# Attention and two quantized convolutions on one core: scores from stacks of two-part k and q, row sums shared with GpSimd, x kept in DRAM

## The chip, the cores and the metric

The kernel runs on one core of a Trainium2 chip. Time is device time in microseconds; lower is better. The engines are TensorE (PE, with its weight loads as PEld), VectorE (DVE), ScalarE (ACT), GpSimd (POOL) and SyncE (SP), which issues most DMAs.

## The reference

The input x is 4 images of 128 channels, 64x64. Layer 0 is self-attention over the 4096 positions of an image, with group norm in front and a residual behind. Layer 1 is a block of two 3x3 convolutions with weights quantized to 3 bits, each followed by batch norm, and a residual:

```python
x_norm = _group_norm(x, norm_w, norm_b)                  # 8 groups
qkv = einsum('oc,bchw->bohw', qkv_w, x_norm) + qkv_b
q, k, v = to_heads(...)                                  # 4 heads of d = 32
attn = softmax(einsum('bhid,bhjd->bhij', q, k) * d ** -0.5)
out = einsum('oc,bchw->bohw', proj_w, einsum('bhij,bhjd->bhid', attn, v)) + proj_b
x = x + out
...
out = relu(batchnorm(conv3x3(x, lsq_quantize(w1, alpha1)), gamma1, beta1))
out = batchnorm(conv3x3(out, lsq_quantize(w2, alpha2)), gamma2, beta2)
return relu(out + x)
```

All arrays are float32.

## The kernel before

*Staging.* All of x stays in SBUF as four padded images `xp` (66x66 a channel). Attention runs over 32 blocks (4 images times 8 blocks of 512 queries), and each block over 32 steps of 128 keys (`kt`). The steps form one long list, so the next block begins where the last one ends.

*A step.* `exp_step` makes the transposed scores of the four heads: four float32 matmuls (L279) with 32 rows of contraction each, the heads lying on different partitions, into two PSUM tiles `s` of two banks (three such tiles exist). In the trace a float32 matmul is two instructions. Two activations (L282) turn them into `p` tiles (128x2048, four buffers). No maximum is subtracted; instead the sums and their reciprocals are checked at the end (`worst`), and a general path would run if they were out of bounds. One step later `av_step` (L289) multiplies p with v into the accumulator `acc`, each head in its own 32 columns.

*Row sums.* `sum_step` (L302) adds the p tiles of four steps on VectorE (three adds of 128x2048), and `ones_step` (L306) sums the result over partitions with a matmul against ones, accumulated over eight groups in `l`.

*The end of a block.* `finish` copies acc and l, takes reciprocals in four pieces (L324), weighs, projects with `wp` (L333) and adds into xp (L335). These run as small tasks, one a step, in the next block (`side_work`).

*Projections.* `project_qkv` makes q, k and v of 512 positions. Image 0 is projected within block 0, and the next image within the last block of the one before. q, k and v stay in SBUF.

*Convolutions.* Bands of 16 rows are split into a high and a low part that float32r holds (L418, L419), and each 512 outputs take 18 float32r matmuls (L428): nine taps times two parts. ScalarE copies PSUM out (L459), VectorE takes the statistics. After the second layer the residual comes from xp (L486).

*Order.* Each engine works through its own list in order. The lists are laid out by a planner in the framework, which may run work ahead of its place in the program where its engine is free: the group norm statistics (L222) of images 1 to 3, called for in later blocks, all run between 17 and 47 us, and the weight quantization (`quant_tasks`, L188 to L202), called for after block 0, between 46.8 us and about 110 us.

Of the kernel before, what the change touches and what calls it, by code (L numbers as in the profile page):

```python
# [22 lines left out]
P = 128  # L23
# [14 lines left out]
GROUPED = 4  # L38
# [40 lines left out]
def _fast_body(ctx, tc, x, norm_w, norm_b, qkv_wt, qkv_b, proj_wt, proj_b,  # L79
# [10 lines left out]
    Q = H // 4  # L90
# [4 lines left out]


    xp = [const.tile([P, H + 2, PW], F32, name=f"xp{b}") for b in range(B)]

    def rows(t, r, n):
        return t[:, 1 + r : 1 + r + n, 1 : 1 + W]  # L100

    for b in range(B):
        for j in range(4):
            eng = nc.sync if b or j % 2 == 0 else nc.scalar
            eng.dma_start(out=rows(xp[b], j * Q, Q), in_=x[b, :, j * Q : (j + 1) * Q, :])

# [34 lines left out]
    for b in range(B):  # L141
        nc.gpsimd.memset(xp[b][:, 0, :], 0.0)
        nc.gpsimd.memset(xp[b][:, H + 1, :], 0.0)
        nc.gpsimd.memset(xp[b][:, 1 : H + 1, 0:1], 0.0)
        nc.gpsimd.memset(xp[b][:, 1 : H + 1, W + 1 : W + 2], 0.0)
# [13 lines left out]
    def quant_tasks(qp):  # L159
        tasks = []  # L160
        for i, (w, alpha) in enumerate(((w1, alpha1), (w2, alpha2))):
# [19 lines left out]
            for c in range(3):  # L181


                def taps(i=i, c=c, w=w, t=t):
                    wr = qp.tile([P, 3, P], F32, name=f"wr{i}{c}", tag="wr")
                    nc.sync.dma_start(out=wr, in_=w[:, 3 * c : 3 * c + 3, :])
                    q0 = qp.tile([P, 3, P], F32, name=f"q0{i}{c}", tag="q0")
                    nc.vector.tensor_scalar(q0, wr, t["inv"], -8.0, ALU.mult, ALU.max)  # L188
                    nc.vector.tensor_scalar(q0, q0, 8.0, None, ALU.min)
                    qh = qp.tile([P, 3, P], F32, name=f"qh{i}{c}", tag="qh")  # L190
                    nc.vector.tensor_scalar(qh, q0, SPLIT, None, ALU.add)
                    nc.vector.tensor_scalar(qh, qh, SPLIT, None, ALU.subtract)
                    ql = qp.tile([P, 3, P], F32, name=f"ql{i}{c}", tag="ql")
# [15 lines left out]
    with ExitStack() as att:  # L209
        qkvp = att.enter_context(tc.tile_pool(name="qkvp", bufs=NB + 1))  # L210
        pex = att.enter_context(tc.tile_pool(name="pex", bufs=2))
        quant = att.enter_context(tc.tile_pool(name="quant", bufs=1))
        pss = att.enter_context(tc.tile_pool(name="pss", bufs=3, space=PSUM))
        psa = att.enter_context(tc.tile_pool(name="psa", bufs=1, space=PSUM))

        norm, qs, ks, vs = {}, {}, {}, {}

        def norm_tasks(b):
            st = small.tile([P, NB, 6], F32, name=f"st{b}", tag="st")

            def stats(j):
                nc.vector.bn_stats(st[:, j, :], rows(xp[b], j * RB, RB))  # L222

            def combine():
                mv = small.tile([P, 2], F32, name=f"mv{b}", tag="mv")
                nc.vector.bn_aggr(mv, st.rearrange("p j s -> p (j s)"))

                gm = pss.tile([P, 2, FB], F32, name=f"gm{b}", tag="s")
                nc.tensor.matmul(gm[:, 0, 0:1], gavg, mv[:, 0:1], start=True, stop=True)
                mean = small.tile([P, 1], F32, name=f"mean{b}", tag="mean")  # L230
                nc.vector.tensor_copy(mean, gm[:, 0, 0:1])
                dv = small.tile([P, 1], F32, name=f"dv{b}", tag="dv")
                nc.vector.tensor_tensor(dv, mv[:, 0:1], mean, ALU.subtract)
                nc.vector.tensor_tensor(dv, dv, dv, ALU.mult)
                nc.vector.tensor_tensor(dv, dv, mv[:, 1:2], ALU.add)
                gv = pss.tile([P, 2, FB], F32, name=f"gv{b}", tag="s")
                nc.tensor.matmul(gv[:, 0, 0:1], gavg, dv, start=True, stop=True)
                r = rsqrt_eps(gv[:, 0, 0:1], f"gr{b}")
                a = small.tile([P, 1], F32, name=f"ga{b}", tag="ga")
                nc.vector.tensor_tensor(a, r, nw, ALU.mult)  # L240
                c = small.tile([P, 1], F32, name=f"gc{b}", tag="gc")
                nc.vector.tensor_tensor(c, mean, a, ALU.mult)
                nc.vector.tensor_tensor(c, nb, c, ALU.subtract)
                norm[b] = a, c

            return [lambda j=j: stats(j) for j in range(NB)] + [combine]
# [3 lines left out]
        def project_qkv(b, j):  # L250
            a, c = norm[b]
            xn = pex.tile([P, FB], F32, name=f"xn{b}_{j}", tag="xn")
            nc.vector.tensor_scalar(xn.rearrange("p (r w) -> p r w", w=W), rows(xp[b], j * RB, RB),  # L253
                                    a, c, ALU.mult, ALU.add)
            ps = pss.tile([P, 2, FB], F32, name=f"pqk{b}_{j}", tag="s")
            nc.tensor.matmul(ps[:, 0, :], wqkv[:, P : 2 * P], xn, start=True, stop=True)  # L256
            nc.tensor.matmul(ps[:, 1, :], wqkv[:, 0:P], xn, start=True, stop=True)
            k = ks[b, j] = qkvp.tile([P, FB], F32, name=f"k{b}_{j}", tag="k")
            q = qs[b, j] = qkvp.tile([P, FB], F32, name=f"q{b}_{j}", tag="q")
            nc.vector.tensor_scalar(k, ps[:, 0, :], bk, None, ALU.add)  # L260
            nc.vector.tensor_scalar(q, ps[:, 1, :], bq, None, ALU.add)  # L261
            ps = pss.tile([P, 2, FB], F32, name=f"pv{b}_{j}", tag="s")
            for i in range(KB):
                nc.tensor.matmul(ps[:, 0, i * P : (i + 1) * P], xn[:, i * P : (i + 1) * P],  # L264
                                 wqkv[:, 2 * P : 3 * P], start=True, stop=True)
            v = vs[b, j] = qkvp.tile([P, KB, P], F32, name=f"v{b}_{j}", tag="v")
            nc.vector.tensor_tensor(v, ps[:, 0, :].rearrange("p (i f) -> p i f", f=P),
                                    bv.unsqueeze(1).to_broadcast([P, KB, P]), ALU.add)
# [3 lines left out]
        def exp_step(blk, kt):  # L272
            b, qb = blk
            q, k = qs[b, qb], ks[b, kt // KB]
            c0 = (kt % KB) * P
            pt = pex.tile([P, HEADS, FB], F32, name=f"p_{b}_{qb}_{kt}", tag="pt", bufs=4)
            s = [pss.tile([P, 2, FB], F32, name=f"s_{b}_{qb}_{kt}_{i}", tag="s") for i in range(2)]
            for h in range(HEADS):
                nc.tensor.matmul(s[h // 2][:, h % 2, :], k[h * D : (h + 1) * D, c0 : c0 + P],  # L279
                                 q[h * D : (h + 1) * D, :], start=True, stop=True)  # L280
            for i in range(2):
                nc.scalar.activation(pt[:, 2 * i : 2 * i + 2, :], s[i], AF.Exp, scale=SCALE)  # L282
            return pt


        def av_step(blk, kt, pt, acc):
            v = vs[blk[0], kt // KB]
            for h in range(HEADS):
                nc.tensor.matmul(acc[h * D : (h + 1) * D, :], v[:, kt % KB, h * D : (h + 1) * D],  # L289
                                 pt[:, h, :], start=(kt == 0), stop=(kt == NK - 1))  # L290
# [3 lines left out]
        def sum_step(blk, kt, pts, sums):  # L294
            n = kt % GROUPED
            if n == 0:
                return
            if n == 1:
                sums[kt // GROUPED] = pex.tile([P, HEADS, FB], F32,
                                               name=f"r_{blk[0]}_{blk[1]}_{kt}", tag="r")  # L300
            r = sums[kt // GROUPED]
            nc.vector.tensor_tensor(r, pts[kt - 1] if n == 1 else r, pts[kt], ALU.add)  # L302

        def ones_step(g, sums, l):
            for h in range(HEADS):
                nc.tensor.matmul(l[h * D : (h + 1) * D, :], ones, sums[g][:, h, :],  # L306
                                 start=(g == 0), stop=(g == NK // GROUPED - 1))

        def finish(blk, acc, sums, l):

            b, qb = blk
            av = pex.tile([P, FB], F32, name=f"av{b}_{qb}", tag="av", bufs=1)
            nc.scalar.copy(av, acc)  # L313
            ls = pex.tile([P, FB], F32, name=f"ls{b}_{qb}", tag="ls", bufs=1)
            rc = pex.tile([P, FB], F32, name=f"rc{b}_{qb}", tag="rc", bufs=1)
            at = pex.tile([P, FB], F32, name=f"at{b}_{qb}", tag="at")

            def last_ones():
                ones_step(NK // GROUPED - 1, sums, l)
                nc.scalar.copy(ls, l)  # L320

            def invert(j):
                cs = slice(j * P, (j + 1) * P)
                nc.vector.reciprocal(rc[:, cs], ls[:, cs])  # L324

            def weigh():
                nc.vector.tensor_tensor(worst, worst, ls, ALU.max)  # L327
                nc.vector.tensor_tensor(worst, worst, rc, ALU.max)  # L328
                nc.vector.tensor_tensor(at, av, rc, ALU.mult)  # L329
# [13 lines left out]
        for t in norm_tasks(0):  # L343
            t()
# [5 lines left out]
        def second(n, kt):  # L350
# [7 lines left out]
            if kt % GROUPED == 2 and kt >= GROUPED:  # L358
                g = kt // GROUPED - 1
                if g == 0:  # L360
                    l[n] = psa.tile([P, FB], F32, name=f"l{n}", tag="l")
# [587 lines left out]
```

## Time and profile before

| what | value |
|---|---|
| time, median of three runs | 3031.2 us (3030.11 to 3031.35) |
| the profiled execution | 3029.39 us, span 3027.6 us |
| TensorE busy | 95% of the span |
| ScalarE, VectorE, GpSimd busy | 69%, 73%, 1% |
| granted TensorE clock, mean | 0.983 |
| copy of acc, first and last block | 161.7 us, 2688.5 us |

The span runs from the first to the last instruction. In lines of groups, the busy time and the mean duration of one instruction stand behind the first bar, and the idle time of the engine just before them, with what ended it, behind the second. In lines in order of time, the first number is the start in us and the second the duration. In lines of stretches, each engine has its busy time and instruction count, in the order PE, PEld, DVE, ACT, POOL, followed by the granted clock, the DMA share and GB/s.

### The profile page before, as it was taken

The page shows a single profiled execution, that of the slowest core. Times are in us where ns is not written, and L with a number is a line of the kernel's source. Part 1 is how long each engine was busy: PE and PEld are TensorE (multiplying, and loading weights), DVE is VectorE, ACT ScalarE, POOL GpSimd, SP SyncE. Part 2 cuts the span into 40 slices and gives each one's busy share as a digit, 9 for nine tenths or more (in the row PEclk, how much of TensorE's full clock was granted, in tenths as well). Part 3 has the DMA queues.
Part 4 walks back from the last instruction along what each step waited for, and adds up shares of the span by engine and source line. Part 5 has one row for each costly group of instructions (what it writes and reads, how often), then busy time and mean ns, then how long its engine had stood idle before and what let it go on. Part 6 is the DMA issues. An engine that isn't in the chain of part 4 may idle for free.

```text
span 3027.6 us, 45635 instructions
## 1 busy us (share of the span) xinstructions
PE 2884.3 (95%) x20050; PEld 928.2 (31%) x20050; DVE 2206.7 (73%) x1475; ACT 2100.7 (69%) x2209; POOL 18.5 (1%) x86
## 2 busy tenths in 40 slices
PE   5899999999999999999999999999999999989895
PEld 2222222223222222222222222232222222237773
DVE  8877777766777777767777777767777777763334
ACT  2488888856888888856888888757888888841223
POOL 1000000000000000000000000000000000000000
PEclk9899999999999999999999999999999999999997
DMA  6000000000000000000000000000000000000002
GB/s 124 9 1 1 1 1 1 1 1 1 1 1 1 1 1 1 1 1 1 1 1 1 1 1 1 1 1 1 1 1 1 1 1 1 1 1 1 1 0 113
DMA packets 36881, 21.30 MB, mean 7 GB/s; under 512 B 33777, under 2 KB 34545, under 8 KB 36673
## 3 DMA queue, kind: packets, MB, share of 16 engines
q1 hardware_dynamic: 32064, 16.91, 2.2%
q8 instruction: 159, 2.61, 0.4%
q10 hardware_dynamic: 4128, 1.05, 0.2%
q0 software_dynamic: 480, 0.33, 0.1%
q14 instruction: 50, 0.40, 0.0%
HBM read 9.90 MB, written 8.39 MB: 6 GB/s over the span
## 4 chain that ended last, share of the span: by engine, by line
PE 63%; DVE 28%; ACT 5%; issue 2%; DMA 1%; SPq 0%; DVEq 0%; POOL 0%; POOLq 0%; ACTq 0%
PE s L279 27%; PE acc L289 21%; DVE r L302 19%; PE ps L428 9%; PE l L306 5%; ACT p L282 5%; DVE rc L324 3%; DVE k L260 1%; DVE q L261 1%; DVE xp L335 1%; DVE at L329 1%; DVE worst L327 1%; DVE worst L328 1%; DMA out_dram<-y 0%; DVE st L222 0%
## 5 line engine op out<-in xcount | busy, mean ns | idle before, releaser
L282 ACT ACTIVATE p<-s 128x1024 f32<-128x1024 f32 x2048 | 1991.7, 1024 | 655.0 <-PE s L279 644.1
L279 PE MATMUL s<-q,k 32*128 32x512 f32 x8192 | 1293.6, 644 | 57.9 <-DVE q L261 47.0
L302 DVE TENSOR_TENSOR r<-r,p 128x2048 f32<-128x2048 f32 x512 | 1171.4, 2288 | 53.2 <-ACT p L282 9.2
L289 PE MATMUL acc<-p,v 128*32 128x512 f32 x8192 | 1100.9, 608 | 7.5 <-ACT av L313 7.5
L302 DVE TENSOR_TENSOR r<-p,p 128x2048 f32<-128x2048 f32 x256 | 586.7, 2292 | 541.8 <-ACT p L282 541.8
L279 PEld LDWEIGHTS s<-q,k 32*128 32x128 f32 x8192 | 411.5, 184 | 921.9 <-issue 548.5
L289 PEld LDWEIGHTS acc<-p,v 128*32 128x32 f32 x8192 | 162.1, 108 | 795.1 <-issue 761.7
L306 PE MATMUL l<-r,ones 128*32 128x512 f32 x2048 | 266.6, 592 | 1.8 <-DVE r L302 1.8
L459 ACT COPY cv<-ps 128x512 f32<-128x512 f32 x64 | 37.6, 588 | 208.3 <-PE ps L428 207.2
L428 PE MATMUL ps<-lo,wq 128*128 128x512 f32 x576 | 151.4, 408 | 11.6 <-DVE lo L419 11.6
L428 PE MATMUL ps<-hi,wq 128*128 128x512 f32 x576 | 148.4, 402 | 0.0
L428 PEld LDWEIGHTS ps<-lo,wq 128*128 128x128 f32 x576 | 110.4, 192 | 41.6 <-issue 12.1
L428 PEld LDWEIGHTS ps<-hi,wq 128*128 128x128 f32 x576 | 109.3, 190 | 29.4
L460 DVE BATCH_NORM_STATS2 st<-cv 128x6 f32<-128x512 f32 x64 | 44.3, 692 | 100.3 <-ACT cv L459 100.3
L306 PEld LDWEIGHTS l<-r,ones 128*32 128x32 f32 x2048 | 66.5, 110 | 155.3 <-issue 151.7
L324 DVE RECIPROCAL rc<-ls 128x128 f32<-128x128 f32 x128 | 108.2, 909 | 1.8 <-ACT ls L320 1.8
L478 ACT ACTIVATE t<-cv,bc,ba 128x1088 f32<-128x1088 f32 (+1 forms) x16 | 21.1, 1328 | 31.5 <-DVE lo L419 27.7
L418 DVE CAST hi<-t 128x1188 fp32r<-128x1188 f32 x16 | 12.5, 778 | 41.1 <-PE ps L428 39.7
L333 PE MATMUL po<-at,wp 128*128 128x512 f32 x64 | 36.9, 660 | 5.4 <-DVE at L329 5.4
L418 DVE CAST hi<-xp 128x1188 fp32r<-128x1188 f32 x16 | 12.3, 776 | 38.7 <-PE ps L428 38.7
L256 PE MATMUL pqk<-xn,wqkv 128*128 128x512 f32 x64 | 37.0, 660 | 3.0 <-DVE xn L253 3.0
L264 PEld LDWEIGHTS pv<-wqkv,xn 128*128 128x128 f32 x256 | 33.7, 192 | 15.6 <-issue 15.3
(98 smaller groups left out, 500.3 us busy)
## 6 DMA issues: line engine op xcount, KB each, us to landing
out_dram<-y SPq DMA_DIRECT2D x16, 512.0 KB, 2.7
xp<-in_x_dram SPq DMA_DIRECT2D x14, 512.0 KB, 7.7
wr<-in_L_conv_w_dram SPq DMA_DIRECT2D x6, 192.0 KB, 2.4
xp<-in_x_dram ACTq DMA_DIRECT2D x2, 512.0 KB, 10.5
wqkv<-in_L_conv_qkv_w_dram POOLq DMA_DIRECT2D x1, 192.0 KB, 6.6
bv<-in_L_conv_qkv_b_dram POOLq DMA_DIRECT2D x1, 64.0 KB, 7.2
wp<-in_L_conv_proj_w_dram POOLq DMA_DIRECT2D x1, 64.0 KB, 6.9
gamma<-in_L_conv_gamma_dram POOLq DMA_DIRECT2D x2, 0.5 KB, 6.5
```

What stands on the lines that cost most here:

```text
L256: nc.tensor.matmul(ps[:, 0, :], wqkv[:, P : 2 * P], xn, start=True, stop=True)
L264: nc.tensor.matmul(ps[:, 0, i * P : (i + 1) * P], xn[:, i * P : (i + 1) * P], wqkv[:, 2 * P : 3 * P], start=True, stop=True)
L279: nc.tensor.matmul(s[h // 2][:, h % 2, :], k[h * D : (h + 1) * D, c0 : c0 + P], q[h * D : (h + 1) * D, :], start=True, stop=True)
L282: nc.scalar.activation(pt[:, 2 * i : 2 * i + 2, :], s[i], AF.Exp, scale=SCALE)
L289: nc.tensor.matmul(acc[h * D : (h + 1) * D, :], v[:, kt % KB, h * D : (h + 1) * D], pt[:, h, :], start=(kt == 0), stop=(kt == NK - 1))
L302: nc.vector.tensor_tensor(r, pts[kt - 1] if n == 1 else r, pts[kt], ALU.add)
L306: nc.tensor.matmul(l[h * D : (h + 1) * D, :], ones, sums[g][:, h, :], start=(g == 0), stop=(g == NK // GROUPED - 1))
L324: nc.vector.reciprocal(rc[:, cs], ls[:, cs])
L333: nc.tensor.matmul(ps[:, 0, :], wp, at, start=True, stop=True)
L428: nc.tensor.matmul(ps, w[:, tap, :], part[:, j * RB + kh : j * RB + kh + RB, kw : kw + W], start=(n == 0), stop=(n == 2 * TAPS - 1))
L459: nc.scalar.copy(dst, ps)
L460: nc.vector.bn_stats(st[:, b * NB + j, :], dst)
```

## The change

*Scores.* q and k are each split into a high and a low float32r part. For each head, k stands four times 32 rows deep as (high, low, high, low) and q as (high, high, low, low), so that one float32r matmul with 128 rows of contraction gives the sum of the four products. A step's scores are four such matmuls.

*Stacks by way of DRAM.* The projection writes the parts and v to DRAM (five stores a chunk of 512 positions), and the stacks are loaded back with the heads side by side: four loads for k and one for v a chunk, four for q a block. All of these are issued by SP.

*Phases.* The program emits scores of three pairs of heads, then the weights of one step, then three more pairs, then the weights of two steps. There are six p buffers.

*Row sums.* In each block p tiles of ten steps (`POOLED`) are added on GpSimd (nine adds), the others on VectorE (21 adds); the two sums meet at step 29 (a 22nd add). The ones product runs once a block. `worst` is kept by GpSimd, with adds in place of maxima.

*Projections.* Chunks of the next image are spread over blocks 2 to 7 of the image before (two in blocks 2 and 3, then one a block), each a few pieces over four steps, in a PSUM bank of their own. Of image 0, three chunks are projected before the first step and five within block 0.

*x in DRAM.* Attention writes its result to DRAM (`y0`), which the first convolution loads back band by band, and the last step again as the residual. x is loaded in chunks where it is needed.

*Ends.* Quantization uses the tiles of the projection's stages and is called for in blocks 1 and 2 of the last image. The first two bands are loaded and split in the last block, and convolved around the finish of it.

```diff
-            for h in range(HEADS):
-                nc.tensor.matmul(s[h // 2][:, h % 2, :], k[h * D : (h + 1) * D, c0 : c0 + P],
-                                 q[h * D : (h + 1) * D, :], start=True, stop=True)
...
+    def scores(pair):
+        step, half = divmod(pair, 2)
...
+        s = pss.tile([P, 2, FB], F32, name=f"s{n}_{kt}_{half}", tag="s")
+        for i in range(2):
+            h = 2 * half + i
+            nc.tensor.matmul(s[:, i, :], k[:, h, c0 : c0 + P], q[:, h, :], start=True, stop=True)
+        nc.scalar.activation(pts[step][:, 2 * half : 2 * half + 2, :], s, AF.Exp, scale=SCALE)
...
+        def parts(what, bias, slot):
+            hi = stage.tile([P, FB], F32R, name=f"{what}h{b}_{j}", tag=f"{what}h")
+            lo = stage.tile([P, FB], F32R, name=f"{what}l{b}_{j}", tag=f"{what}l")
+            nc.vector.tensor_scalar(hi, ps[what], bias, None, ALU.add)
+            nc.vector.scalar_tensor_tensor(lo, ps[what], bias, f32(hi), ALU.add, ALU.subtract)
+            nc.sync.dma_start(out=kq[b, j][slot], in_=f32(hi))
+            nc.sync.dma_start(out=kq[b, j][slot + 1], in_=f32(lo))
...
+    def load_stack(t, b, j, slots):
+        for s, slot in enumerate(slots):
+            nc.sync.dma_start(
+                out=f32(t)[s * D : (s + 1) * D, :, :],
+                in_=kq[b, j][slot].rearrange("(h d) n -> d h n", d=D))
+
+    def load_kv(b, j):
+        ks[b, j] = stack_tile(f"k{b}_{j}")
+        load_stack(ks[b, j], b, j, (0, 1, 0, 1))
+        v = vs[b, j] = vpool.tile([P, KB, P], F32, name=f"v{b}_{j}", tag="v")
+        nc.sync.dma_start(out=v.rearrange("p i f -> p (i f)"), in_=kq[b, j][4])
...
+    POOLED = (1, 2, 4, 7, 10, 13, 16, 19, 22, 25)
+    MERGE = 29
...
+        if kt in POOLED:
+            if kt == POOLED[1]:
+                psum[n] = rpool.tile([P, HEADS, FB], F32, name=f"rp{n}", tag="rp")
+                nc.gpsimd.tensor_tensor(psum[n], pts[step - 1], pt, ALU.add)
+            elif kt > POOLED[1]:
+                nc.gpsimd.tensor_tensor(psum[n], psum[n], pt, ALU.add)
+        elif kt == 3:
+            rsum[n] = rpool.tile([P, HEADS, FB], F32, name=f"r{n}", tag="r")
+            nc.vector.tensor_tensor(rsum[n], pts[step - 3], pt, ALU.add)
+        elif kt > 3:
+            nc.vector.tensor_tensor(rsum[n], rsum[n], pt, ALU.add)
+        if kt == MERGE:
+            nc.vector.tensor_tensor(rsum[n], rsum[n], psum[n], ALU.add)
...
+        def weigh():
+            nc.vector.tensor_tensor(av, av, rc, ALU.mult)
+            nc.gpsimd.tensor_tensor(worst, worst, t["ls"], ALU.add)
+            nc.gpsimd.tensor_tensor(worst, worst, rc, ALU.add)
...
+        def store():
+            nc.vector.scalar_tensor_tensor(t["x"], t["o"], bp, t["x"], ALU.add, ALU.add)
+            nc.sync.dma_start(out=y0[b][:, qb * FB : (qb + 1) * FB], in_=t["x"])
...
+        if n + 1 < len(blocks) and qb < NB - 1:
+            add(2, "", lambda: load_q(b, qb + 1))
...
+            for j, kt in {2: ((0, 13), (1, 22)), 3: ((2, 13), (3, 22)), 4: ((4, 15),),
+                          5: ((5, 15),), 6: ((6, 15),), 7: ((7, 15),)}.get(qb, ()):
...
+                chunk(b + 1, j, kt, project_parts(b + 1, j, lambda xt=xt: xt[0]), False)
...
+    run_scores(2)
+    while at["step"] < steps:
+        for s, w in ((3, 1), (3, 2)):
+            run_scores(s)
+            run_weights(w)
...
+    def load_band(b, g):
+        raw[b, g] = t = band_tile(f"t0_{b}_{g}")
+        inner, lo, hi = border(t, g)
+        nc.sync.dma_start(out=inner, in_=y0[b].rearrange("p (h w) -> p h w", w=W)[:, lo:hi, :])
...
+            r = outs.tile([P, Q], F32, name=f"r{b}_{j}", tag="r")
+            nc.sync.dma_start(out=r, in_=y0[b][:, cs])
             y = outs.tile([P, Q], F32, name=f"y{b}_{j}", tag="y")
-            nc.vector.scalar_tensor_tensor(y, cv[b][:, j * Q : (j + 1) * Q, :], a2,
-                                           rows(xp[b], j * Q, Q), ALU.mult, ALU.add)
+            nc.vector.scalar_tensor_tensor(y, cv[b][:, cs], a2, r, ALU.mult, ALU.add)
```

## The prediction

> **What bounds the kernel now.** I read the busy shares first, then the slices, the groups, the order of time in one block, and the stretches by engine. All sums are made against the profiled execution: span 3027.6 us, 3029.4 us with what lies around it, 1.8 us under the median of 3031.2 us. I take 3.6 us as the step from a span to a median; 0.2% (6 us) is about what a measurement of this kernel can tell from no change.
>
> Busy shares and slices:
>
> ```profile
> PE 2884.3 (95%) x20050; PEld 928.2 (31%) x20050; DVE 2206.7 (73%) x1475; ACT 2100.7 (69%) x2209; POOL 18.5 (1%) x86
> ...
> PE   5899999999999999999999999999999999989895
> ...
> ACT  2488888856888888856888888757888888841223
> ```
>
> TensorE is full; ScalarE dips every ninth slice, between two batches; GpSimd does nothing. The groups (line, engine, busy us, mean ns, idle before them):
>
> ```profile
> L282 ACT ACTIVATE p<-s 128x1024 f32<-128x1024 f32 x2048 | 1991.7, 1024 | 655.0 <-PE s L279 644.1
> L279 PE MATMUL s<-q,k 32*128 32x512 f32 x8192 | 1293.6, 644 | 57.9 <-DVE q L261 47.0
> L302 DVE TENSOR_TENSOR r<-r,p 128x2048 f32<-128x2048 f32 x512 | 1171.4, 2288 | 53.2 <-ACT p L282 9.2
> ```
>
> ScalarE waits for scores (644 us). One step in order of time (start, duration):
>
> ```profile
> 217.19 1.14 PE L279 MATMUL s<-q,k 32*128 32x512 f32 x8
> 218.26 1.06 PE L289 MATMUL acc<-p,v 128*32 128x512 f32 x8
> 219.25 1.31 PE L279 MATMUL s<-q,k 32*128 32x512 f32 x8
> ```
>
> Scores 1.07, weights 0.99; ones add 0.97 in one step of four. A steady block, and one that projects the next batch:
>
> ```profile
> 161.70:239.10 77.40, 76.78 (x582) 20.02 (x578) 60.45 (x32) 63.08 (x67) 0.00 (x0) 1.00 0.00 1
> 628.00:746.00 118.00, 109.42 (x672) 35.51 (x666) 78.71 (x62) 63.72 (x67) 0.00 (x0) 0.97 0.00 1
> ```
>
> PE, its loads, DVE, ACT, POOL: 77.4 us with PE at 76.8; three blocks of about 118 us carry 3 x 40.6 = 122 us of projections. The copies of acc place the rest: block 0 ends at 161.7, the last at 2688.5, and 339.1 us of finish, convolutions and output follow. The 31 blocks between average 81.5 us.
>
> **The change part by part.**
>
> *Scores.* A step's eight instructions at 1.07 us become four one-pass products. The nearest row is the convolution, also fp32r over 128 rows, with a weight load each: nine start every 2.15 us.
>
> ```profile
> 2717.63 2.32 PE L428 MATMUL ps<-lo,wq 128*128 128x512 f32 x9
> 2719.78 2.31 PE L428 MATMUL ps<-hi,wq 128*128 128x512 f32 x9
> ```
>
> So 0.239 each, 0.956 a step. Over three steps: 12 x 0.239 = 2.87; weights 0.99 + 0.99 where scores follow, 0.89 where weights follow (215.33 to 216.22 has no change of form) = 2.87. The drain from a 128-row product into the weights isn't shown: 0 to 0.2, twice. 5.74 to 6.14 per three steps, so 61 to 66 a block.
>
> *Ones.* Eight groups become one: 7 x 0.97 = 6.8 us leave PE.
>
> *Projections.* 2.8 us of PE a chunk (656.03 to 658.83), now one a block on average, plus ones 1.0 and wp 1.1: PE needs 66 to 71 us a block. ScalarE, two exps per 1.94 us and two copies of 0.59, needs 63.3. With three score buffers and phases they cannot dovetail fully: 66 to 74, I take 70.
>
> *Row sums.* DVE: 24 adds become 21 and the merge, 22 x 2.29 = 50.4. Four reciprocals 3.6, av 0.69, residual 0.75, statistics 0.69, and per chunk 0.54 + 4 x 0.75 + 0.68 = 4.2 (the hi and lo passes): 60.3 us in all. Nine adds of 128x2048 go to POOL. No row prices one. Below: 2.29, were POOL as fast as DVE. Above: POOL's affine_select of 128x128 took 0.36 against 0.10 for 128x1 memsets, 2.05 ns an element of one input; doubled for two inputs, 8.5. I take the row itself, 2048 x 2.05 + 0.1 = 4.3 us: 38.7 a block; the two 512-wide adds into worst, 1.15 each, 2.3: 41 us. The Trainium skill (GPSIMD Engine Reference, 3.1) measures 4497 ns for this add and would make it 42.8.
>
> POOL's 41 us fit under 70, if POOL and DVE run side by side. The trace has one place that speaks on this: POOL memsets of 18 elements, 0.13 us in the open, but not while DVE casts:
>
> ```profile
> 2850.14 0.77 DVE L418 CAST hi<-t 128x1188 fp32r<-128x1188 f32 x1
> ...
> 2850.37 0.61 POOL L470 MEMSET t<- 128x18 f32 x1 [4.48 <-DVE lo L419]
> ...
> 2854.61 0.13 POOL L470 MEMSET t<- 128x18 f32 x1 [1.42 <-DVE lo L419]
> ```
>
> The first ends at 2850.98, 0.07 us after the cast (2850.91); the same at 2852.49. So the two engines share a way into SBUF, and one waits out the other's whole instruction. The memset then ended inside the next DVE TENSOR_TENSOR: that one lets POOL write. Whether it lets POOL read is not shown: POOL reads nothing beside such an add here. But the cast reads 1188 elements in 0.78 us and the TENSOR_TENSOR 2 x 1188 in 1.38: the same rate, as if by the same two paths. By that nearest row I take it that a DVE add and a POOL add exclude each other; the other end, no contact, is kept. The Trainium skill (SBUF — State Buffer, Who interferes with whom) says so outright: a DVE instruction with two SBUF inputs contends with a GpSimd one that reads SBUF, and whoever comes second waits for the whole of the first; the trace agrees for the cast, and no run here shows the add. By the rule alone, at the page's 4497 ns, the block is 98 us; without it 70.
>
> Taken in turns, a block needs 50.4 + 0.7 + 41 = 92; DVE's other 9 us hide in POOL's turns only when they stand at the head of its queue, say half: 97 us. Behind a waiting DVE add stand the chunk's hi/lo passes, the reciprocals and the residual, for which PE and SP wait; behind a waiting POOL add only the next. Both hold p buffers: six, so ScalarE stops when the adds are three or four steps late.
>
> *DRAM.* A block adds some 18 issues on SP, 0.33 us each (the output's stores): 6 us; 4.5 MB in 70 us or more is 64 GB/s, against 212 GB/s at the start, and loads come a block ahead. SP is in order; behind a load waiting for a k buffer stand the next q and residual, due 20 steps later: nothing. The first scores gain a store and a load, 2 x 2.7: at 32 us instead of 27. Bands of x (256-byte runs, 2.5 us to issue, 7.7 to land) hide behind the 8.6 us that a band convolves, two ahead.
>
> *Quantization.* 42 us of DVE lay in block 0 (46.8 to 103). It moves or is planned early again: 21 us in turns, half hidden.
>
> *End.* Two bands convolve beside the last finish: the 13.8 us from 2688.5 to 2702.3 go. The residual, once in SBUF, is 16 loads of 512 KB: 8.4 MB went out in 30 us, so 12 loads not yet in cost 22 us. Bounds: 0, and +54 if each load queues behind the store before it (16 x (2.7 + 1.28 + 1.15) = 82, against 28). Tail 339 - 14 + 22 = 347. Border memsets lie on POOL, idle there.
>
> *Sum.* 32 + 32 x 97 = 3104 + 10 (five chunks in block 0, 21 us of DVE, half hidden) + 21 + 347 = 3514; at the median, 3518. I say 3515.
>
> **The rivals.**
>
> *Side by side* (the other side). POOL's adds cost DVE nothing. 32 + 32 x 70 + 14 (five chunks on PE) + 22 (quantization over DVE's 10 us of slack in two blocks) + 347 = 2655; with 66 to 74, 2530 to 2785. It decides at (3027.6 - 410)/32 = 81.8 us a block, 12 over the free pace: 56 + 41f = 81.8, so when less than f = 0.63 of POOL's time is lost to DVE. For: POOL is idle, and the memset ran beside the TENSOR_TENSOR. Against: the equal read rates.
>
> *Shared by the element.* The path alternates and neither waits out an instruction. If half of POOL's 41 us hides, 56 + 20 = 76, up to 56 + 34 = 90: 2860 to 3290, either sign. For: the memset needed only the cast's end. Against: it waited for the whole of it.
>
> *The planner undoes the phases.* Engine order is planned (statistics of batches 1 to 3 already ran at 17 to 47 us). Alternating every step costs 0.1 to 0.3 us a step, 3 to 10 us a block: 2750 to 2980 without contact; nothing in turns.
>
> **How the numbers follow.** In turns 0.57; shared by the element 0.15, half of it faster; side by side, phases kept or not, 0.28. Faster 0.28 + 0.07 = 0.35, same 0.01, slower 0.64. In turns alone: 3350 to 3680 (block 92 to 102). Eight in ten must reach into side by side: 2620 to 3680 leaves out about a tenth at each end.
>
> **What would show it.** Right: DVE adds far over 2.29 us or with gaps that end at POOL's, POOL busy over 40 us a block, PE and ACT near 65% in all slices, blocks near 97 us. Score products starting every 0.24 us and no 118 us blocks hold in either case. Wrong if POOL and DVE adds overlap at their own lengths, or blocks stay under 80 us.

## The result, and the profile after

The changed kernel takes 3635.4 us (median of four runs, 3635.16 to 3635.71) against 3030.8 us before (four runs): 1.1995 times the time, 95% interval 1.1974 to 1.2016. The profiled execution is 3635.68 us, its span 3634.0 us at a mean granted clock of 0.909 (0.983 before).

Busy shares and three of the slice rows of the page of after:

```profile
PE 3014.7 (83%) x14162; PEld 1259.9 (35%) x14162; DVE 3159.2 (87%) x1411; ACT 2062.7 (57%) x2209; POOL 1748.3 (48%) x462
...
DVE  5999989997998989998998999998999999996333
ACT  2665566665665565665665566566556666661122
POOL 3554565564554555555554455555544556561000
```

The full engine is VectorE now, in every slice of the attention, with GpSimd about half busy beside it. ScalarE's dips at every ninth slice are gone: the projections are spread, as the change says. But its level is 5 to 6 tenths instead of 8.

The groups of the page of after (busy us, mean ns, then idle time before them):

```profile
L341 ACT ACTIVATE p<-s 128x1024 f32<-128x1024 f32 x2048 | 1950.1, 1032 | 1142.5 <-PE s L340 938.2
L364 DVE TENSOR_TENSOR r<-r,p 128x2048 f32<-128x2048 f32 x640 | 2367.2, 3699 | 117.9 <-ACT p L341 88.8
L359 POOL TENSOR_TENSOR rp<-rp,p 128x2048 f32<-128x2048 f32 x256 | 1374.4, 5369 | 706.2 <-ACT p L341 703.8
L340 PE MATMUL s<-q,k 128*128 128x512 f32 x4096 | 1285.7, 437 | 114.5 <-ACT p L341 101.3
...
L362 DVE TENSOR_TENSOR r<-p,p 128x2048 f32<-128x2048 f32 x32 | 102.8, 3213 | 103.5 <-ACT p L341 60.9
```

The same DVE add, with the same shapes, that took 2288 ns before has a mean of 3699. The 640 adds of L364 lie between 2219 and 6689 ns, with a median of 2293; 241 are over 2.5 us (minimum/median/maximum ns, first and last start in us):

```profile
L364 DVE TENSOR_TENSOR r<-r,p x640: 2219/2293/6689, 59.3 to 3293.7; 128x2048 f32<-128x2048 f32 x160
```

The chain that ended last, by engine and by line (shares of the span):

```profile
DVE 54%; PE 26%; issue 13%; ACT 4%; DMA 2%; POOL 1%; DVEq 0%; SPq 0%; POOLq 0%; ACTq 0%
```

and some of its longest pieces in order of time (start, us):

```profile
28.02 9.27 DMA kq<-kh
181.87 6.60 DVE r L364
...
1813.71 6.67 DVE r L364
1847.38 6.51 DVE r L364
```

The path runs through the long adds. Here is one stretch in order of time, VectorE and then GpSimd in the trace of after (start, duration):

```profile
1796.29 6.19 DVE L364 TENSOR_TENSOR r<-r,p 128x2048 f32<-128x2048 f32 x1
...
1803.27 5.81 DVE L364 TENSOR_TENSOR r<-r,p 128x2048 f32<-128x2048 f32 x1
...
1809.87 2.22 DVE L364 TENSOR_TENSOR r<-r,p 128x2048 f32<-128x2048 f32 x1
```

```profile
1795.74 4.59 POOL L359 TENSOR_TENSOR rp<-rp,p 128x2048 f32<-128x2048 f32 x1
1801.95 4.98 POOL L359 TENSOR_TENSOR rp<-rp,p 128x2048 f32<-128x2048 f32 x1 [1.62 <-ACT p L341]
1810.02 3.22 POOL L394 TENSOR_TENSOR worst<-worst,rc 128x512 f32<-128x512 f32 x1 [3.09 <-DVE rc L389]
```

Work out the ends. The first GpSimd add ends at 1800.33; the DVE add that began inside it ends at 1802.48, 2.15 us later, one whole add. The second GpSimd add began at 1801.95, while that DVE add still ran, and ends at 1806.93, 4.45 us after the DVE add's end, again about one whole add. The DVE add of 1803.27 ends at 1809.08, 2.15 after GpSimd's end. And the other way round: the small GpSimd add of 1810.02 ends at 1813.24, 1.15 after the DVE add of 1809.87 does (1812.09). Whoever comes second waits out the whole of the first, in both directions. Over the whole trace, of 710 TENSOR_TENSORs of DVE longer than 2 us, the 304 that meet no GpSimd instruction have a mean of 2.29 us, the 406 that meet one 4.62.

### The profile page after: what moved, and what is told of

Its sections match the earlier page's. It is cut to its first block, busy times and chain, and to the rows that moved or that the text cites. A ratio compares the mean times of both kernels' runs of the same rounds, so it can differ in the third digit from the quotient of the medians.

```text
span 3634.0 us, 35912 instructions
## 1 busy us (share of the span) xinstructions
PE 3014.7 (83%) x14162; PEld 1259.9 (35%) x14162; DVE 3159.2 (87%) x1411; ACT 2062.7 (57%) x2209; POOL 1748.3 (48%) x462
## 4 chain that ended last, share of the span: by engine, by line
DVE 54%; PE 26%; issue 13%; ACT 4%; DMA 2%; POOL 1%; DVEq 0%; SPq 0%; POOLq 0%; ACTq 0%
DVE r L364 46%; PE acc L352 8%; PE c L584 7%; PE s L340 7%; ACT p L341 3%; DVE r L362 2%; DVE r L366 1%; PE pq L280 1%; PE l L382 1%; DVE rc L389 1%; PE pv L293 1%; DMA r<-y 0%; DVE kl L286 0%; POOL rp L359 0%; DVE y L681 0%
## 5 line engine op out<-in xcount | busy, mean ns | idle before, releaser
L364 DVE TENSOR_TENSOR r<-r,p 128x2048 f32<-128x2048 f32 x640 | 2367.2, 3699 | 117.9 <-ACT p L341 88.8
L359 POOL TENSOR_TENSOR rp<-rp,p 128x2048 f32<-128x2048 f32 x256 | 1374.4, 5369 | 706.2 <-ACT p L341 703.8
L340 PE MATMUL s<-q,k 128*128 128x512 f32 x4096 | 1285.7, 437 | 114.5 <-ACT p L341 101.3
L352 PE MATMUL acc<-p,v 128*32 128x512 f32 x8192 | 1380.6, 633 | 0.0
L340 PEld LDWEIGHTS s<-q,k 128*128 128x128 f32 x4096 | 723.6, 197 | 1082.9 <-ACT p L341 601.7
L357 POOL TENSOR_TENSOR rp<-p,p 128x2048 f32<-128x2048 f32 x32 | 169.6, 5301 | 565.4 <-ACT p L341 413.6
L362 DVE TENSOR_TENSOR r<-p,p 128x2048 f32<-128x2048 f32 x32 | 102.8, 3213 | 103.5 <-ACT p L341 60.9
L584 PE MATMUL c<-lo,wq 128*128 128x512 f32 x576 | 152.1, 408 | 9.5 <-DVE lo L433 8.1
L382 PE MATMUL l<-r,ones 128*32 128x512 f32 x256 | 51.8, 868 | 121.2 <-DVE r L364 121.2
L584 PE MATMUL c<-hi,wq 128*128 128x512 f32 x576 | 149.0, 403 | 0.0
```

Source lines behind the costliest of these rows:

```text
L340: nc.tensor.matmul(s[:, i, :], k[:, h, c0 : c0 + P], q[:, h, :], start=True, stop=True)
L352: nc.tensor.matmul(acc[n][h * D : (h + 1) * D, :], v[:, kt % KB, h * D : (h + 1) * D], pt[:, h, :], start=(kt == 0), stop=(kt == NK - 1))
L357: nc.gpsimd.tensor_tensor(psum[n], pts[step - 1], pt, ALU.add)
L359: nc.gpsimd.tensor_tensor(psum[n], psum[n], pt, ALU.add)
L362: nc.vector.tensor_tensor(rsum[n], pts[step - 3], pt, ALU.add)
L364: nc.vector.tensor_tensor(rsum[n], rsum[n], pt, ALU.add)
```

## The experiments

The theory on record was "in turns": a two-input DVE add and a GpSimd add exclude each other, and their sum sets the block. Its rivals were that they run side by side and something else is slow, that they share by the element, and that the planner, which lays out each engine's order, breaks up the phases on PE. "Block" below is the mean distance between copies of acc. It is 81.5 us before and 100.9 after.

### What makes the adds long

**No adds on GpSimd.** The ten steps of `POOLED` are left out of the row sums, and so is the merge:

```diff
         if kt in POOLED:
-            if kt == POOLED[1]:
-                psum[n] = rpool.tile([P, HEADS, FB], F32, name=f"rp{n}", tag="rp")
-                nc.gpsimd.tensor_tensor(psum[n], pts[step - 1], pt, ALU.add)
-            elif kt > POOLED[1]:
-                nc.gpsimd.tensor_tensor(psum[n], psum[n], pt, ALU.add)
+            pass
...
-        if kt == MERGE:
-            nc.vector.tensor_tensor(rsum[n], rsum[n], psum[n], ALU.add)
```

> The nine POOL adds and the merge left out (ten tiles of a block are missing from the row sums), the 21 DVE adds stay. In turns: DVE adds at 2.29 us, DVE 58 us a block, the pace falls to what PE and ScalarE allow, 68 to 74 us a block, 2600 to 2780 us. If the stacks, phases or DRAM are what costs: blocks stay over 85 us and the time over 3150.

Measured: 2923.6 us, 0.9654 of before [0.9635, 0.9673]. The DVE adds are at 2.29 us again and the block is 78.5 us. The group of adds in this run:

```profile
L360 DVE TENSOR_TENSOR r<-r,p 128x2048 f32<-128x2048 f32 x640 | 1468.2, 2294 | 342.7 <-ACT p L341 324.1
```

So the GpSimd adds and the merge together are worth 3635.4 - 2923.6 = 712 us, more than the whole loss of 605. But 78.5 is above the 68 to 74 that was expected of a free block; the next section takes that up.

**GpSimd writes only.** Each GpSimd add becomes two memsets of the same tile (the sums of those tiles are lost; GpSimd stays busy for 3.64 us instead of 4.59):

```diff
-                nc.gpsimd.tensor_tensor(psum[n], psum[n], pt, ALU.add)
+                nc.gpsimd.memset(psum[n], 0.0)
+                nc.gpsimd.memset(psum[n], 0.0)
```

> Each POOL add replaced by two memsets of the same 128x2048 tile, so that POOL writes as much but reads nothing (the row sums lack ten tiles); the DVE adds and the merge stay. If a two-input DVE add excludes only a POOL instruction that reads: DVE adds stay at 2.29 us, blocks at 70 to 76, 2640 to 2820 us. If any POOL work in SBUF excludes it: DVE adds average over 3 us and the time stays over 3200.

Measured: 2949.5 us, 0.9739 [0.972, 0.9759], block 79.2. The groups of this run:

```profile
L366 DVE TENSOR_TENSOR r<-r,p 128x2048 f32<-128x2048 f32 x640 | 1468.1, 2294 | 330.5 <-ACT p L341 311.1 <-DVE r L366 0.5 <-ACT av L378 0.5
L361 POOL MEMSET rp<- 128x2048 f32 x256 | 466.1, 1821 | 12.8
```

GpSimd is busy for 1200.7 us of this run, and the DVE adds keep 2294 ns (12 of 640 are over 2.5 us). A busy GpSimd isn't what costs; one that only writes passes a two-input DVE add. It doesn't pass every DVE instruction: the normalization of a chunk (`xn<-x`, one 128x512 tile from SBUF), 0.54 us by itself, takes up to 2.09 us here:

```profile
L276 DVE TENSOR_SCALAR xn<-x,ga,gc x24: 536/680/2089, 228.7 to 1849.6; 128x512 f32<-128x512 f32 x24
```

Why this run takes 26 us more than the one before, which also lacks the merge, was not tested.

**DVE reads one input.** 20 of the 21 adds of DVE become reductions of p alone, into four columns (the sums of those tiles are then wrong); GpSimd adds as in the changed kernel:

```diff
-            nc.vector.tensor_tensor(rsum[n], rsum[n], pt, ALU.add)
+            nc.vector.tensor_reduce(rsum[n][:, :, 0], pt, AX.X, ALU.add)
```

> POOL's nine adds stay; 20 of the 21 DVE adds become reductions of the same p tile along its rows into four columns (one SBUF input, the same 2048 elements; the row sums are left out). In turns by the read path: the reductions keep their own length, 2.2 to 2.4 us, POOL's adds fall to 4.2 to 4.6 us beside them, blocks at 70 to 78, 2640 to 2860 us. If POOL and DVE exclude each other whatever DVE reads, or if POOL's adds are that slow by themselves: POOL adds stay over 5 us, or DVE's over 3, and the time over 3300.

Measured: 2998.2 us, 0.99 [0.988, 0.992], block 81.0. That is above the range expected, with PE as the bound again (83% of its chain). Its groups:

```profile
L364 DVE TENSOR_REDUCE r<-p 128x4 f32<-128x2048 f32 x640 | 1458.0, 2278 | 288.3 <-ACT p L341 268.5 <-DVE r L364 0.9
L359 POOL TENSOR_TENSOR rp<-rp,p 128x2048 f32<-128x2048 f32 x256 | 1192.3, 4657 | 547.3 <-ACT p L341 545.7
```

```profile
L359 POOL TENSOR_TENSOR rp<-rp,p x256: 4497/4589/6522, 55.7 to 2637.5; 128x2048 f32<-128x2048 f32 x128
```

The reductions read the same tiles in the same time as the adds (2278 ns, at most 2293) and meet GpSimd's adds without a loss on either side: GpSimd's add now has a median of 4.59 us, its own length. Together the two runs name the resource: DVE's second input and GpSimd's reads. One thing more changed with the reductions: they write four columns where the adds write 2048. That DVE's writes are not what collides can be seen in the trace of after. The residual `x<-po,bp,x` (L404) reads one tile from PSUM and one from SBUF and writes all 512 columns; 13 of its 32 instructions begin while a GpSimd add runs, and the longest of the 32 takes 751 ns:

```profile
L404 DVE SCALAR_TENSOR_TENSOR x<-po,bp,x x32: 737/739/751, 188.4 to 3305.9; 128x512 f32<-128x512 f32 x32
```

DVE's second input and GpSimd's reads are also what the Trainium skill names (SBUF — State Buffer, Who interferes with whom): a DVE instruction with two SBUF inputs contends with a GpSimd one that reads, not with one that only writes, and a reduction never contends. The runs here agree on all three, with 3699 against 2294 and 2278 ns. One SBUF input alone doesn't make a DVE instruction safe, though. In the trace of after 12 of the 24 normalizations (L276) begin while GpSimd adds and take 1.48 to 4.81 us; the other 12 take 0.53 to 0.55:

```profile
L276 DVE TENSOR_SCALAR xn<-x,ga,gc x24: 532/1012/4807, 256.8 to 2338.3; 128x512 f32<-128x512 f32 x24
```

So this instruction collides with GpSimd's adds and with its memsets, as the cast of the trace before did with a memset. What sets it apart from the reduction was not tested.

**GpSimd reads one input.** Each GpSimd add becomes a copy of p (the sums again lost):

```diff
-                nc.gpsimd.tensor_tensor(psum[n], psum[n], pt, ALU.add)
+                nc.gpsimd.tensor_copy(psum[n], pt)
```

> The changed kernel with each POOL add replaced by a POOL copy of the p tile into rp: POOL reads one tile instead of two and writes as much (the row sums are wrong by it). The memsets of e3 took 1.8 us, so the copy takes at least that; two of the adds' inputs took 4.58, so at most about 4.5. If any POOL instruction that reads SBUF and a two-input DVE add exclude each other: DVE adds at two lengths again, mean over 2.7 us, and blocks at 51 + 9 x (1.8 to 4.5) + 7 = 75 to 98 us, at least 2780 us. If only a POOL instruction with two inputs does: DVE adds all at 2.29 us, 2900 to 2960 us as in e3.

Measured: 2962.6 us, 0.978 [0.9761, 0.98], block 79.9. The instructions of the two lines (minimum/median/maximum ns, first and last start in us):

```profile
L359 POOL COPY rp<-p x256: 1886/2314/4062, 55.5 to 2601.8; 128x2048 f32<-128x2048 f32 x128
```

```profile
L364 DVE TENSOR_TENSOR r<-r,p x640: 2220/2292/4000, 57.6 to 2622.9; 128x2048 f32<-128x2048 f32 x160
```

The longest of either is close to 1.9 + 2.3, one whole instruction of the other, so a single GpSimd input excludes a DVE add as two do. It costs less: a copy holds the way for 1.9 us instead of 4.6, and 130 of the 640 DVE adds are over 2.5 us instead of 241. The mean of the 640 is 2.52, less than the 2.7 expected, and PE is the full engine again (95%), so that much of the waiting costs no time.

### What the planner's order costs

The run without GpSimd adds is 139 us above the top of what the prediction gave for side by side (2785). PE in order of time in the run without GpSimd adds:

```profile
1828.86 1.65 PE L340 MATMUL s<-q,k 128*128 128x512 f32 x6
1830.44 1.93 PE L352 MATMUL acc<-p,v 128*32 128x512 f32 x16
1832.29 1.67 PE L340 MATMUL s<-q,k 128*128 128x512 f32 x6
1833.90 1.06 PE L352 MATMUL acc<-p,v 128*32 128x512 f32 x8
1834.89 1.19 PE L340 MATMUL s<-q,k 128*128 128x512 f32 x4
1836.02 1.04 PE L352 MATMUL acc<-p,v 128*32 128x512 f32 x2
1836.99 0.73 PE L340 MATMUL s<-q,k 128*128 128x512 f32 x2
1837.66 1.92 PE L352 MATMUL acc<-p,v 128*32 128x512 f32 x14
1839.50 1.64 PE L340 MATMUL s<-q,k 128*128 128x512 f32 x6
```

The first two rows are a round as the program emits it: six score products, the weights of two steps (16 instructions, two for each head), 3.43 us to the next scores. From 1834.89 on one head's weights (two instructions) have slipped ahead of the third pair of scores: 4.61 us to the next round (1839.50) for the same work. One head takes 0.97 us, and eight instructions of four heads no more (0.99, 1833.90 to 1834.89): the heads, each in its own 32 columns, run beside each other only when they follow one another.

**The order held, without GpSimd adds.** The run without GpSimd adds, with an order-only edge (no wait on the chip) from every score or weight matmul to the next. The same edit, here and at the weights, is in every run that is said to hold the order:

```diff
+    def keep(m):
+        if chain:
+            tc.add_manual_dep(m.ins, chain[0].name, mybir.DependencyInfo(
+                mybir.DependencyClass.NoSync, mybir.DependencyReason.DATA), reason="order")
+        chain[:] = [m.ins]
...
-            nc.tensor.matmul(s[:, i, :], k[:, h, c0 : c0 + P], q[:, h, :], start=True, stop=True)
+            keep(nc.tensor.matmul(s[:, i, :], k[:, h, c0 : c0 + P], q[:, h, :], start=True, stop=True))
```

> e2 (POOL's adds left out) with TensorE's score and weight matmuls held in the order that the program writes: three pairs, one step, three pairs, two steps. In e2 the planner slipped one head's weights in before the third pair: 1.13 + 0.98 + 0.66 + 1.85 = 4.62 us where six products and two whole steps take 1.58 + 1.85 = 3.43, in some 250 of 341 rounds. If those split steps are what e2 lost to 70 us a block: 1.2 x 250 = 300 us off, 2600 to 2680. If it lost it to DRAM, projections or the phases themselves: within 60 us of 2924.

Measured: 2735.7 us, 0.9031 [0.9013, 0.9049], block 72.4. The order is worth 188 us, some 6 us a block; the weights' time on PE, from each start to PE's next, fell from 38.3 to 32.0 us a block and the scores' stayed (35.6 and 36.2). The time is still above the expected 2600 to 2680: 128 products in 36.2 us, waits among them, are 0.283 each, not 0.239.

**The changed kernel with the order held.**

```diff
-            nc.tensor.matmul(acc[n][h * D : (h + 1) * D, :], v[:, kt % KB, h * D : (h + 1) * D],
-                             pt[:, h, :], start=(kt == 0), stop=(kt == NK - 1))
+            keep(nc.tensor.matmul(acc[n][h * D : (h + 1) * D, :], v[:, kt % KB, h * D : (h + 1) * D],
+                                  pt[:, h, :], start=(kt == 0), stop=(kt == NK - 1)))
```

> The changed kernel itself, with TensorE's order held. If its pace is set by DVE and POOL taking turns: block 95 to 102 us as before, 3480 to 3660, DVE adds still at two lengths, 2.3 and about 6 us. If the split steps on TensorE share in it, as in e1: under 3400.

Measured: 3637.5 us, 1.2009 [1.1985, 1.2033], block 101.05. Nothing is won: in the changed kernel the adds set the pace, and PE has time for a bad order.

**All adds on DVE.** 31 adds on VectorE and none on GpSimd:

```diff
-        if kt in POOLED:
...
+        if kt == 1:
+            rsum[n] = rpool.tile([P, HEADS, FB], F32, name=f"r{n}", tag="r")
+            nc.vector.tensor_tensor(rsum[n], pts[step - 1], pt, ALU.add)
+        elif kt > 1:
             nc.vector.tensor_tensor(rsum[n], rsum[n], pt, ALU.add)
```

> All 31 adds of a block on VectorE, none on GpSimd (its two 512-wide adds into worst stay). In turns (a two-input DVE add and a POOL add exclude each other): DVE is alone, adds return to 2.29 us each, 31 x 2.29 = 71 and 10 of its other work = 81 to 83 us a block; with the first block and the tail of the changed kernel 3000 to 3090 us, some 570 below it, although DVE has nine adds more. If the time lies elsewhere (phases, DRAM traffic, planner): DVE carries 9 x 2.29 = 20 us more a block and the kernel gets slower than 3635.

Measured: 3404.7 us, 1.1243 [1.1225, 1.1262], block 93.8, far above the range expected. The adds kept their 2290 ns; PE was the full engine (96%), because here the planner split the weights of about half of the steps: 540 groups of two instructions for 1024 steps. (The expectation of the next run says "nearly every step"; the trace doesn't show so many.) It also broke most of the score products into groups of two. Groups, then PE in order of time, in this run:

```profile
L358 DVE TENSOR_TENSOR r<-r,p 128x2048 f32<-128x2048 f32 x960 | 2198.2, 2290 | 67.4 <-ACT p L341 13.7 <-DVE r L358 2.3 <-ACT av L368 0.5
```

```profile
1814.87 1.04 PE L352 MATMUL acc<-p,v 128*32 128x512 f32 x2
1815.85 0.73 PE L340 MATMUL s<-q,k 128*128 128x512 f32 x2
1816.51 1.06 PE L352 MATMUL acc<-p,v 128*32 128x512 f32 x6
1817.50 0.73 PE L340 MATMUL s<-q,k 128*128 128x512 f32 x2
```

Two instructions take 0.98 us and six 0.99: the weights of such a step are paid twice.

**All adds on DVE, the order held.** The edits of the last two runs together:

```diff
+        elif kt > 1:
             nc.vector.tensor_tensor(rsum[n], rsum[n], pt, ALU.add)
...
+            keep(nc.tensor.matmul(s[:, i, :], k[:, h, c0 : c0 + P], q[:, h, :], start=True, stop=True))
```

> e1 (all adds on VectorE) in the same held order. If e1's 3405 instead of 3050 was the order of TensorE, which ran one head's weights apart from three in nearly every step: DVE becomes the bound, 82 to 85 us a block, 3020 to 3130, so the kernel of before within 3%. If it was something else: over 3300.

Measured: 3123.3 us, 1.0306 [1.0289, 1.0324], block 84.4, within the range expected. Against the changed kernel with the order held, this is what it costs to give the nine adds of a block to GpSimd instead of VectorE, with PE's order the same: 3637.5 - 3123.3 = 514 us. GpSimd's help costs more than the work that it takes over. Now DVE's 31 adds bound, as the chain of this run has it (by engine):

```profile
DVE 62%; PE 23%; issue 8%; ACT 4%; DMA 2%; DVEq 0%; POOL 0%; SPq 0%; ACTq 0%; POOLq 0%
```

### Versions without GpSimd

**Six groups of row sums.** No GpSimd work in a block; the ones product runs once for each of six groups, and VectorE adds its 128x512 result from PSUM (about 0.68 us), so 26 large adds remain; the order is held, `worst` is kept by VectorE:

```diff
+    ENDS = (5, 10, 16, 19, 25, 31)
+    FLUSH = (9, 12, 18, 21, 27)
...
+    def ones_group(n, g):
+        l = psa.tile([P, FB], F32, name=f"l{n}_{g}", tag="m")
+        for h in range(HEADS):
+            keep(nc.tensor.matmul(l[h * D : (h + 1) * D, :], ones, rsum[n, g][:, h, :],
+                                  start=True, stop=True))
...
+            nc.vector.tensor_tensor(lsum[n], lsum[n], l, ALU.add)
```

> A version meant to beat both: no sums on POOL, the row sums in six groups a block, 26 adds on VectorE instead of 31, each group's ones product added into a tile of its own from PSUM (0.69 us), worst back on VectorE, and the same held order. DVE 26 x 2.29 + 3.5 + 11 = 74, PE 66 to 71 + 5 x 0.95 = 71 to 76: 75 to 80 us a block, 2820 to 2980 us, 2 to 7% under the kernel of before. If row sums can't be had without POOL and without more PE time, at or over 3030.

Measured: 2986.2 us, 0.9859 [0.9842, 0.9875], block 79.9: below the time before, and 6 us above the range expected. PE is at 92%, DVE at 82%. The chain of this run, by engine:

```profile
PE 82%; DVE 10%; ACT 3%; issue 3%; DMA 2%; SPq 0%; POOL 0%; DVEq 0%; POOLq 0%; ACTq 0%
```

**Four groups.** Two ones products fewer, two DVE adds more:

```diff
-    ENDS = (5, 10, 16, 19, 25, 31)
-    FLUSH = (9, 12, 18, 21, 27)
+    ENDS = (7, 15, 23, 31)
+    FLUSH = (10, 18, 26)
```

> e7 with four groups of eight steps instead of six: PE two ones products less, 2 x 0.97, DVE two adds more and two ones sums less, 2 x (2.29 - 0.69) = 3.2 us a block. If PE bounds e7's block of 79.9 us: 78 us, 2920 to 2960. If DVE does: 83 us, 3050 to 3100. If both share it: within 1% of 2986.

Measured: 2951.2 us, 0.9736 [0.972, 0.9752], block 78.9. Busy shares of this run:

```profile
PE 2705.3 (92%) x14930; PEld 1223.7 (41%) x14930; DVE 2560.2 (87%) x1763; ACT 2035.7 (69%) x2209; POOL 26.0 (1%) x110
```

Its chain, by engine:

```profile
PE 59%; DVE 27%; issue 7%; ACT 5%; DMA 2%; SPq 0%; DVEq 0%; POOL 0%; POOLq 0%; ACTq 0%
```

This beats both kernels, by 2.6% and 18.8%. More work for DVE and less for PE made it faster, so PE was the tighter limit with six groups. The block fell by 1.0 us of the 1.9 that left PE, and DVE's share of the chain rose from 10% to 27%: with four groups the two engines are nearer to level. This version has the change's stacks, phases, spread projections and x in DRAM. It differs in three things: the row sums (without GpSimd, in four groups), `worst` on VectorE, and the order of PE held.

## Why the prediction was right, and where its sizes were off

Predicted were 3515 us, from 2620 to 3680; measured 3635. The likeliest case, "in turns" (3350 to 3680), is what happened.

**The mechanism holds.** "A DVE add and a POOL add exclude each other" is confirmed by the ends of the adds in both directions, and by the runs that took away one reader or the other. The step that led there from the trace before, though, was partly luck. The read rates called equal are not quite so (1188 elements in 0.78 us are 1.52 a ns, 2376 in 1.38 are 1.72), and the row shows a cast that holds up a memset, where a two-input add lets a memset pass, as the run with memsets shows. So *side by side* (2655) and *shared by the element* (2860 to 3290) are both out: a held-up add runs its whole length after the other's end, and the reductions and memsets show what the path is. The point that was to decide between faster and slower, 81.8 us a block, is consistent with every run: below it (72.4 to 81.0) all were faster than before, above it (84.4 to 101.05) all slower.

**The sum, term by term.** It fell 120 us short of the profiled span: 14 in the first block, 100 in the 31 that follow (the quantization's 21 counted with them), 5 in the tail.

- *The turns, 92 us; measured 91.9.* For so long in a block a two-input add of DVE or a GpSimd add runs. But the agreement is two errors. GpSimd's add was put at 4.3 us, from the rate of another instruction, and takes 4.59 by itself (the run with reductions; the shortest of the changed kernel 4495 ns). That the estimate came so near was luck, since a GpSimd copy, with one input, takes 1.89. An add into worst takes about 1.27 instead of 1.15. By these the sum is 22 x 2.29 + 9 x 4.59 + 2 x 1.27 + 0.69 = 94.9. Against that, an instruction that waited ends some 0.14 us sooner after the other than its own length (2.15 for 2.29, 4.45 for 4.59, 1.15 for about 1.27 above), as if a little of its start were done while it waits; at up to two handovers for each of 11 GpSimd adds that makes 3 us, worked out here and not tested. The Trainium skill's 4497 ns (GPSIMD Engine Reference, 3.1) is nearer to the 4.59 than the estimate was.
- *Beside the turns, 5 us and 0.7 of quantization; measured 9.05.* VectorE does its other work in 4.9 of these, so "say half" held. The other 4.1 us it waits, and the sum has no term for that: this is the step that failed. In the groups of after, VectorE idles 117.9 us before L364 and 103.5 before L362, 6.9 us a block, mostly for p; the part of it in which GpSimd doesn't add either is lost.
- *First scores at 32 us; measured 38.9.* The sum had 2.7 us each for a store and a load. The first chunk's store lands in 2.0 us, but the second's (kq<-kh, 9.27 us in the chain above) was issued behind the nine loads of the first stacks, and the third chunk's kh waits for it before the first scores start. With the first block the miss is 14 us (acc copied at 153.3, predicted 139).
- *Tail 347; measured 352.1.* Not taken apart further.

**The free pace was wrong, though nothing in the result shows it.** The block without contact was taken at 70 us, 66 to 74. It is 78.5 as the planner lays it out, 72.4 with the order held. There were two errors. The score product, put at 0.239 us by the convolution's row, takes 0.283 on average even with the order held. And the planner does undo phases. That rival was priced at 3 to 10 us a block and 2750 to 2980 us without contact: measured 6.1 (78.5 against 72.4), 9.4 with all adds on DVE (93.8 against 84.4), and 2923.6 us. "Nothing in turns" holds as well: 3637.5 against 3635.4.

**What was to show it.** Long adds: seen. GpSimd over 40 us a block: seen (56 us in the first steady block, since an instruction that waits counts as busy). No blocks of 118 us: right, they lie between 92.3 and 114.5. ACT near 65%: 57. PE near 65% was wrong: 83%. With the order held it is still 78%, where the score and weight products alone are busy for 1288 + 1166 us, against 979 each in the sum (2.87 us for three steps, 341 times). This stretch of the changed kernel (PE, its loads, DVE, ACT, POOL, then granted clock) has PE nearly as full as DVE:

```profile
153.30:245.60 92.30, 81.72 (x397) 31.06 (x398) 87.53 (x36) 61.34 (x66) 56.05 (x11) 0.94 0.12 30
1795.00:1895.00 100.00, 88.66 (x424) 32.89 (x426) 92.78 (x41) 65.02 (x70) 59.51 (x14) 0.93 0.07 17
```

Split weights fill PE's spare time, and the granted clock is lower in the kernels in which PE is busy less (0.909 at 83% in the changed kernel, 0.882 at 78% with the order held, 0.983 at 96% without GpSimd adds). Busy time on PE was thus no sign of PE at its limit.

## What to carry to other kernels

Before work is given to an idle engine, ask which way into SBUF it shares: an add on GpSimd held up two-input VectorE adds for its whole 4.59 us to save 2.29, while a memset there beside such adds, or a one-input reduction on VectorE beside GpSimd's adds, cost nothing. Try it with the very instructions: another one-input VectorE instruction, the normalization, waited in both cases. Read such a contact from the ends: an instruction that ends one whole length of its own after the other's end waited for it, although both count as busy. And when a program emits phases, read PE's instructions in order of time to see whether they survived the planning; here holding them was worth 188 us, but only once nothing slower covered it.

## What the runs showed that was not expected

- One head's weights, in 32 columns, take TensorE 0.97 us; four heads in a row take 0.99. A group broken up by other matmuls is paid twice.
- A GpSimd copy, with one input, excludes a DVE add as an add with two inputs does (copies of L359: longest 4062 ns, shortest 1886; DVE adds of L364: longest 4000 ns, median 2292).
- A GpSimd memset of 128x2048 takes 1.82 us beside DVE adds at 2294 ns: neither is held up. But a normalization of one 128x512 tile on VectorE, 0.54 us alone, takes up to 2.09 us beside such memsets and up to 4.81 beside GpSimd adds.
- Six score products in a row take 1.58 us after a change of form (0.263 each), where nine products of the convolution took 2.15 (0.239 each).
